# Two layers of cross-attention: three of the six key chunks scored with the keys on the partitions

## The chip, the cores and the metric

The kernel runs on one core of a Trainium2 chip. A NeuronCore has five engines that run side by side and meet through semaphores: PE multiplies matrices (its weight loads are listed apart, as PEld), DVE does elementwise work and reductions, ACT does the exponentials and some copies, POOL issues the stores here, and SP issues the loads. Transfers run on 16 DMA engines. The metric is the device time of one execution in microseconds (us); shorter is better.

## The reference

Two cross-attention layers follow one another over the same context. x is (8, 100, 640), the context is (8, 722, 1024), of which 77 tokens are "text" and 645 are "image" tokens; there are 20 heads of width 32. What one layer computes, for each batch element and head:

```
q = x @ Wq ;  k, v = text @ Wk, text @ Wv ;  ki, vi = image @ Wk_ip, image @ Wv_ip
out_text = softmax(q k^T / sqrt(32)) v
out_ip   = softmax(q ki^T / sqrt(32) [+ 0.5 * sem]) vi   [* mask]
x        = (out_text + out_ip) @ Wo + bo + x
```

What stands in brackets belongs to the second layer alone: sem is a score of the image tokens that all heads share, and mask is a factor for each query row. Everything is float32. Two softmaxes, one over 77 keys and one over 645, are weighted and added.

## The kernel before

**Visits.** A unit u is one batch element of one layer: u = 0 to 7 are the first layer (`B` = 8), 8 to 15 the second. A unit has five chunks c of four heads (4 x 32 = 128 rows of q and k). The main loop, which begins at L1328, makes one visit for each (u, c), 80 in all; the first 40 are the first layer's. A visit makes the scores of its own heads and finishes the heads of the visit before, called `last`.

**Scores (L980).** The 722 keys of a head come in two parts: 512 image keys (`KA`), then 133 image keys and 77 text keys (`KB` = 210 columns). `scores(u, c, 0)` stands at the start of a visit, `scores(u, c, 1)` in its middle. Each makes four matmuls, one for each head, with the head's 32 rows of q as weights and its keys as the moving operand (L992): queries (100) lie on the partitions, keys along the free axis. Four PSUM banks in two tiles `sc0` and `sc1` take them. DVE then takes the maxima (L1001), for part 1 also the text maxima and the shifted text scores (L1022, L1023) and the differences of the two parts' maxima (L1029, L1030). ACT takes the exponentials with their row sums (L1015, two records for each), for part 1 also those of the differences and of the text (L1033, L1034). `factors` on DVE (L1037 to L1041) makes what each part is to be multiplied with, 1/Z included; ACT multiplies the first 512 keys (L1047, one for each head), DVE the remaining ones (L1055 image, L1051 text). The result p of a visit is [100 queries, 4 heads, 722 keys] in SBUF, two buffers.

**Transposes and values.** Before p can be multiplied with v, the keys have to be on the partitions. `transposes` (L1086) does that for one of six chunks of keys j: four transposes on PE into a PSUM bank (L1096), then one copy into `pt`, on DVE (L1103) for j = 0, 1, 3, 5 and on ACT (L1101) for j = 2 and 4. `values` (L1105) makes 24 matmuls with v as weights (L1119) and copies the sum into `hs` (L1123).

**Production.** Between these steps the kernel makes the k and v of later units from the context, by a scheme of seven products instead of eight (`seven`): products a to e go into two PSUM buffers (`ps_pj`), and each is added up by DVE (L207, L217, L222, L228, L233) or copied by ACT (L202, L211). PE can begin a product only when the one that used its buffer two steps earlier has been read. The matmuls are L637 (v) and L667 (k).

**Order.** PE, DVE and ACT run their instructions in the order in which the program writes them (`PINNED`); SP's and POOL's order is left to the scheduler of the framework. `spread` (L1190) gives each production task a place on an axis on which a visit has length 1, from the task's own cost and from a visit's "own" time (5.3 plus small pieces). `between(n, a, b, small)` in the main loop then makes those due between two steps of the visit: 0 to 0.4 before the first two transposes, 0.4 to 0.6 before the next two and part 1, 0.6 to 0.8 before the last two, then the rest. What DVE and ACT do after the maxima is held back in a list `later`; `next_task` (L1298) writes out one entry of it ahead of each production task that has a cost, and the visit's end writes out what is left, ahead of `values`. So in each engine's queue these entries stand between the evictions of production products.

**Loads.** `load_k` fetches the [128, 722] tile of a visit's keys (L507, L508; two buffers), `load_v` its values (L513; two buffers), `load_x` the context (L174), `load_wo` the weights of the output pieces (L895), all on SP.

Of the kernel before, what the change touches and what calls it, by code (L numbers as in the profile page):

```python
# [9 lines left out]
F32 = mybir.dt.float32  # L10
AF = mybir.ActivationFunctionType
ALU = mybir.AluOpType
# [3 lines left out]
B = 8  # L16
# [11 lines left out]
NC_ = C // P  # L28
NCC = CC // P
NTAIL = NL + NT  # L30
SCALE = 1.0 / math.sqrt(D)
SEM_SCALE = 0.5
NU = 2 * B
# [13 lines left out]
def two_layer_xattn(  # L47
# [35 lines left out]
    k_d = [dram.tile([P, NC_, NI], F32, tag=f"k_{u}", name=f"k_d{u}") for u in range(NU)]  # L83
    v_d = [dram.tile([NB * P, C], F32, tag=f"v_{u}", name=f"v_d{u}") for u in range(NU)]
    g_d = [dram.tile([2, NI, NT], F32, tag=f"g_{g}", name=f"g_d{g}") for g in range(B // 2)]

    ident = const.tile([P, P], F32, tag="ident", name="ident")
    make_identity(nc, ident)
# [876 lines left out]
        nc.sync.dma_start(out[LAST[i] % B], resg[g][:, i])  # L965


    pr, stats, sct = {}, {}, {}

    later = []  # L970

# [5 lines left out]

        emit(max([i + 1 for i, (r, _) in enumerate(later) if r], default=0))

    def scores(u, c, part):  # L980
        k0, k1 = ((0, KA), (KA, NK))[part]
        if part == 0:
            pr[u, c] = ppool.tile([S, 4, NK], F32, tag="p", name=f"p_{u}_{c}")

            stats[u, c] = stat.tile([S, 14, 4], F32, tag="st", name=f"st_{u}_{c}")
        else:
            free_scores()

        scs = [ps_sc.tile([P, 2, 512], F32, tag=f"sc{h}", name=f"sc_{u}_{c}_{part}_{h}") for h in range(2)]
        for i in range(4):  # L990
            rows = slice(32 * i, 32 * i + 32)
            nc.tensor.matmul(  # L992
                scs[i // 2][:S, i % 2, : k1 - k0], lhsT=qs_[u][rows, c, :], rhs=ks[u, c][rows, k0:k1], start=True, stop=True
            )
        p, st, l = pr[u, c], stats[u, c], u // B
        n = min(k1, NI) - k0
        lo, f, rz, mul = st[:, 6, :], st[:, 7:9, :], st[:, 9:11, :], st[:, 11:13, :]

        def maxima(h):
            if l == 0:  # L1000
# [31 lines left out]
        def text_exponentials():  # L1032
            nc.scalar.activation(f, f, AF.Exp)  # L1033
            nc.scalar.activation(p[:, :, NI:], p[:, :, NI:], AF.Exp)  # L1034
# [14 lines left out]
        def scaled_rest(text):  # L1049
# [4 lines left out]
            else:  # L1054
# [2 lines left out]
                    ALU.mult,  # L1057
                )

        for h in range(2):  # L1060
            maxima(h)
        if part == 0:
            later.append((True, lambda: exponentials(0)))
            later.append((True, lambda: exponentials(1)))
        else:
            for h in range(2):
                text_maxima(h)
            differences()
            later.append((True, lambda: (exponentials(0), exponentials(1), text_exponentials())))
            if (u, c) == ORDER[-1]:  # L1070

                later.append((False, lambda: (
                    factors(), scaled((0, 1)),
                    nc.vector.tensor_tensor(
                        p[:, 2:, :KA], p[:, 2:, :KA], mul[:, 0, 2:].unsqueeze(2).to_broadcast([S, 2, KA]), ALU.mult
                    ),
                    scaled_rest(False), scaled_rest(True),
                )))
                return
            later.append((False, lambda: (factors(), scaled_rest(False))))  # L1080
            later.append((False, lambda: (scaled((0, 1)), scaled_rest(True))))
            later.append((False, lambda: scaled((2, 3))))

    pts = {}

    def transposes(u, c, j, at_end=False):  # L1086
        if j == 0:
            emit(len(later))
            pts[u, c] = one.tile([P, 6, 4 * S], F32, tag="pt", name=f"pt_{u}_{c}")
        rows = P if j < 5 else NTAIL  # L1090
        if at_end and j in (2, 3):
            ps = ps_sc.tile([P, 2, 512], F32, tag=f"sc{j - 2}", name=f"pspt_{u}_{c}_{j}")[:, 0]
        else:
            ps = ps_pt.tile([P, 512], F32, tag="pt", name=f"pspt_{u}_{c}_{j}")
        for i in range(4):
            nc.tensor.transpose(  # L1096
                ps[:rows, i * S : (i + 1) * S], pr[u, c][:, i, j * P : j * P + rows], ident[:S, :S]
            )
        dst, src = pts[u, c][:rows, j, :], ps[:rows, : 4 * S]
        if j in (2, 4) or at_end and j == 0:  # L1100
            nc.scalar.copy(dst, src)  # L1101
        else:
            nc.vector.tensor_copy(dst, src)  # L1103

    def values(u, c):  # L1105
        g, at = group_of[u]
        if g not in hsg:

            hsg[g] = one.tile([P, 2, NC_, S], F32, tag="hs" if g < len(PAIRS) - 1 else "qst", name=f"hs_{g}")
        pt = pts[u, c]  # L1110
        ps = ps_pt.tile([P, 512], F32, tag="pt", name=f"pv_{u}_{c}")
        for j in range(6):
            for i in range(4):
                if j < 5:
                    lhs = vs[u, c][:, j, i * D : (i + 1) * D]
                else:
                    lhs = vts[u][:, (4 * c + i) * D : (4 * c + i + 1) * D]
                rows = P if j < 5 else NTAIL
                nc.tensor.matmul(  # L1119
                    ps[32 * i : 32 * i + 32, :S], lhsT=lhs, rhs=pt[:rows, j, i * S : (i + 1) * S],  # L1120
                    start=(j == 0), stop=(j == 5),
                )
        nc.vector.tensor_copy(hsg[g][:, at, c, :], ps[:, :S])  # L1123


    AHEAD = 1.2
# [63 lines left out]
    def spread(a, b, tasks):  # L1190

        parts = [(max(a, n), min(b, n + 1)) for n in range(math.floor(a), math.ceil(b))]
        own = [(hi - lo) * (5.3 + small_time(math.floor(lo))) for lo, hi in parts]
        total = sum(t for t, _ in tasks)
        level = (total + sum(own)) / (b - a)
        while True:
            room = [max(0.0, level * (hi - lo) - o) for (lo, hi), o in zip(parts, own)]
            if sum(room) <= total * 1.001:
                break
            level *= 0.999  # L1200
        placed, done, i, before = [], 0.0, 0, 0.0
        scale = sum(room) / total
        for t, f in tasks:
            at = done * scale
            while i < len(parts) - 1 and at >= before + room[i]:
                before += room[i]
                i += 1
            lo, hi = parts[i]
            placed.append((t, lo + (hi - lo) * min(1.0, (at - before) / max(room[i], 1e-9)), f))
            done += t  # L1210
        return placed
# [74 lines left out]
    with tc.manual_schedule(engines=PINNED):  # L1286
# [45 lines left out]
        for n, (u, c) in enumerate(ORDER):  # L1332
# [3 lines left out]
            if n == len(ORDER) - 1:  # L1336
                load_v(*last)
                load_v(u, c)
            between(n, 0.0, 0.4, at[0])
            if last:  # L1340
                transposes(*last, 0)
                transposes(*last, 1)
            between(n, 0.4, 0.6, at[1])
            if last:
                transposes(*last, 2)
                transposes(*last, 3)
            scores(u, c, 1)
            if n == NC_ * LAST[0] - 1:
                load_q(LAST[1])
            few = n >= NC_ * LAST[0] + 4  # L1350
            if not few:
                between(n, 0.6, 0.8, at[2])
            if n < len(ORDER) - 2:
                load_v(u, c)
            if n + 1 < len(ORDER):
                load_k(*ORDER[n + 1])
            if last:
                transposes(*last, 4)
                transposes(*last, 5)
            if few:  # L1360
                between(n, 0.6, 0.8, at[2])
# [58 lines left out]
```

## Time and profile before

| | |
|---|---|
| median of 3 runs | 2047.27 us (2047.24 to 2047.77) |
| the profiled execution | 2048.29 us, of which its trace spans 2046.5 us |
| granted PE clock | 0.998 of full speed |
| PE, PE weight loads, DVE, ACT busy over the span | 99%, 77%, 55%, 38% |
| first visit's scores to those of the 41st (the first layer's visits) | 405.3 to 1338.8 us |
| PE transposes, all visits | 1920, 252 ns each by the records |

A record's duration for PE includes the time in which it overlaps the next one, so a group is better read by the time from its first start to the next group's first start; eight transposes take 0.69 us so. An fp32 matmul of the program shows as two records (a transpose as one). A wait in the table of waits is the idle time of an engine just before an instruction, put down to what ended it. DVE's and ACT's idle time costs nothing by itself as long as PE goes on.

### The profile page before, as it was taken

What the parts mean: (1) busy time and instruction counts of PE and PEld (TensorE: products, weight loads), DVE (VectorE), ACT (ScalarE), POOL (GpSimd) and SP (SyncE); (2) the same over time, 40 slices, a digit from 0 to 9 for tenths busy, and PEclk for the clock granted to TensorE, in tenths of its full rate; (3) what the DMA queues carried; (4) which work ended last, traced back from release to release, by engine and by line L of the source; (5) the groups of instructions that cost most, each with busy time, mean ns of one, the idle gap of its engine ahead of it and who ended that gap; (6) DMA issues with size and microseconds to landing.
All of it is one profiled execution on the core that took longest, in us unless ns stands there. A gap on an engine that the chain in (4) does not pass through costs nothing.

```text
span 2046.5 us, 38708 instructions
## 1 busy us (share of the span) xinstructions
PE 2027.1 (99%) x15162; PEld 1573.3 (77%) x15162; DVE 1130.6 (55%) x3047; ACT 783.0 (38%) x2245; POOL 274.1 (13%) x433
## 2 busy tenths in 40 slices
PE   9999999999999999999999999999999999999998
PEld 9676768776876867778678777777777778888877
DVE  2223322246555455554657665656665667778787
ACT  1001000033433343333434344444543545556675
POOL 0001212111111101111111001001011111111110
PEclk9999999999999999999999999999999999999999
DMA  9544323323432533225245353326332535555461
GB/s 343 151 135 147 102 75 93 99 74 90 117 99 74 155 95 110 86 89 166 79 136 162 106 155 113 95 91 180 107 106 89 152 105 152 161 141 139 124 184 52
DMA packets 296484, 252.20 MB, mean 123 GB/s; under 512 B 46638, under 2 KB 265442, under 8 KB 296302
## 3 DMA queue, kind: packets, MB, share of 16 engines
q1 hardware_dynamic: 274254, 181.19, 31.9%
q0 software_dynamic: 21776, 68.44, 9.2%
q8 instruction: 119, 1.95, 0.4%
q14 instruction: 63, 0.52, 0.1%
q10 hardware_dynamic: 272, 0.10, 0.0%
HBM read 180.74 MB, written 68.93 MB: 122 GB/s over the span
## 4 chain that ended last, share of the span: by engine, by line
PE 95%; DVE 4%; ACT 1%; issue 0%; DMA 0%; SPq 0%; DVEq 0%
PE psv_a L637 9%; PE psv_d L637 8%; PE pspt L1096 8%; PE psk_a L667 8%; PE psk_d L667 7%; PE sc L992 6%; PE pv L1119 4%; PE psv_e L637 4%; PE psk_b L667 4%; PE psk_c L667 4%; PE psv_b L637 4%; PE psv_c L637 4%; PE psk_e L667 4%; PE pso L904 3%; PE psq L923 2%; PE psq L305 2%
## 5 line engine op out<-in xcount | busy, mean ns | idle before, releaser
L1015 ACT ACTIVATE p<-sc,st 100x512 f32<-100x512 f32 (+1 forms) x320 | 165.5, 529 | 202.3 <-DVE st L1001 120.5
L1047 ACT ACTIVATE p<-p,st 100x512 f32<-100x512 f32 x318 | 206.7, 713 | 50.9 <-DVE st L1041 50.6
L1096 PEld LDWEIGHTS pspt<-ident,p 100*128 100x128 f32 (+1 forms) x1920 | 189.0, 138 | 43.3 <-issue 5.5
L1103 DVE COPY pt<-pspt 128x400 f32<-128x400 f32 (+1 forms) x319 | 175.3, 568 | 83.8 <-PE pspt L1096 75.3
L1096 PE MATMUL pspt<-ident,p 100*128 100x100 f32 (+1 forms) x1920 | 211.5, 252 | 6.8 <-DVE pt L1103 2.1
L1015 ACT ACTIVATE p<-p,st 100x512 f32<-100x512 f32 (+1 forms) x320 | 176.6, 554 | 78.2 <-DVE st L1007 78.1
L637 PE MATMUL psv_a<-wv,x 128*128 128x397 f32 (+1 forms) x560 | 185.8, 474 | 0.6 <-DVE ko L228 0.3
L1101 ACT COPY pt<-pspt 128x400 f32<-128x400 f32 x161 | 79.1, 491 | 268.4 <-PE pspt L1096 268.0
L637 PE MATMUL psv_d<-wv,s 128*128 128x320 f32 (+1 forms) x560 | 174.5, 454 | 0.0
L691 POOL DMA_DIRECT2D k_d<-ko x140 | 100.0, 718 | 453.5 <-DVE ko L228 399.8
L637 PEld LDWEIGHTS psv_a<-wv,x 128*128 128x128 f32 x560 | 103.2, 190 | 68.5 <-issue 13.3
L1007 DVE CUSTOM_DVE_ANT_0 p<-sc,sem 100x512 f32<-100x512 f32 (+1 forms) x320 | 138.7, 490 | 21.9 <-PE sc L992 21.0
L637 PEld LDWEIGHTS psv_d<-wv,s 128*128 128x128 f32 x560 | 103.8, 190 | 51.8 <-issue 2.5
L1001 DVE TENSOR_REDUCE st<-sc 100x2 f32<-100x1024 f32 (+1 forms) x160 | 125.3, 824 | 28.8 <-PE sc L992 28.7
L992 PE MATMUL sc<-k,q 32*100 32x210 f32 (+1 forms) x1280 | 138.6, 502 | 0.0
L667 PE MATMUL psk_d<-s,wk 128*128 128x256 f32 (+1 forms) x672 | 136.7, 349 | 0.1
L667 PE MATMUL psk_a<-x,wk 128*128 128x256 f32 (+1 forms) x672 | 135.2, 346 | 0.0
L667 PEld LDWEIGHTS psk_d<-s,wk 128*128 128x128 f32 x672 | 108.6, 189 | 20.6 <-issue 6.7
L667 PEld LDWEIGHTS psk_a<-x,wk 128*128 128x128 f32 x672 | 109.6, 189 | 17.6 <-issue 4.5
L652 POOL DMA_DIRECT2D v_d<-vo x70 | 38.8, 554 | 624.6 <-DVE gst L627 318.6
L637 PE MATMUL psv_e<-wvt,x 128*128 128x397 f32 (+1 forms) x280 | 92.9, 474 | 0.0
L1119 PEld LDWEIGHTS pv<-pt,v 128*32 128x32 f32 x3200 | 67.7, 110 | 26.0 <-issue 16.3
(218 smaller groups left out, 3306.0 us busy)
## 6 DMA issues: line engine op xcount, KB each, us to landing
x<-ip_t SPq DMA_DIRECT2D x80, 512.0 KB
k<-k_d SPq DMA_DIRECT2D x80, 322.5 KB
v<-v_d SPq DMA_DIRECT2D x80, 320.0 KB
v_d<-vo POOLq DMA_DIRECT2D x70, 320.0 KB, 2.4
k_d<-ko POOLq DMA_DIRECT2D x112, 128.0 KB, 4.1
o<-wo SPq DMA_DIRECT2D x35, 320.0 KB
x<-ip_t SPq DMA_DIRECT2D x20, 532.0 KB
q<-wq SPq DMA_DIRECT2D x20, 320.0 KB
```

What stands on the lines that cost most here:

```text
L637: nc.tensor.matmul(ps[:, :m], lhsT=tokens(k)[:, :P], rhs=w[:, k, :], start=(k == 0 and not go_on), stop=(k == HK - 1), skip_group_check=True,)
L667: nc.tensor.matmul(ps[:, i * m : (i + 1) * m], lhsT=w[:, k, :], rhs=tokens(k), start=(i == 0 and k == 0 and not go_on), stop=(k == HK - 1) ...
L691: nc.gpsimd.dma_start(dst[:, :, r], src)
L992: nc.tensor.matmul(scs[i // 2][:S, i % 2, : k1 - k0], lhsT=qs_[u][rows, c, :], rhs=ks[u, c][rows, k0:k1], start=True, stop=True)
L1001: nc.vector.tensor_reduce(st[:, part, 2 * h : 2 * h + 2], scs[h][:S, :, :n], AX.X, ALU.max, negate=True)
L1007: nc.vector.tensor_tensor_reduce(out=p[:, i, k0 : k0 + n], in0=scs[h][:S, i % 2, :n], in1=sems[u][:, k0 : k0 + n], scale=-1.0, scalar=3.0e ...
L1015: nc.scalar.activation(dst, dst if l else scs[h][:S, i % 2, :n], AF.Exp, bias=st[:, part, i : i + 1], scale=-1.0 if l else 1.0, accum_out= ...
L1047: nc.scalar.activation(p[:, i, :KA], p[:, i, :KA], AF.Copy, scale=mul[:, 0, i : i + 1])
L1096: nc.tensor.transpose(ps[:rows, i * S : (i + 1) * S], pr[u, c][:, i, j * P : j * P + rows], ident[:S, :S])
L1101: nc.scalar.copy(dst, src)
L1103: nc.vector.tensor_copy(dst, src)
L1119: nc.tensor.matmul(ps[32 * i : 32 * i + 32, :S], lhsT=lhs, rhs=pt[:rows, j, i * S : (i + 1) * S], start=(j == 0), stop=(j == 5),)
```

## The change

In the first layer, key chunks j = 0, 1, 2 (the first 384 keys, `KT` = 3) are no longer transposed. After part 1 of the next visit's scores, PE makes the scores of `last` for these 384 keys a second time with the operands swapped: k as weights (32 rows x 128 keys), q as the moving operand, so that the keys lie on the partitions (`key_scores`, 12 matmuls). They go into the columns 210 to 509 of the four banks that part 1 of the current heads uses. DVE adds the negative maximum of each query (`key_exponentials`, two instructions) and ACT takes the exponential (two), in place, in `pt`. These come ahead of the current heads' own exponentials in `later`.

The maximum lies along the partitions' other axis, so it goes through DRAM: `finished` writes the smaller of the two negative maxima and 1/Z of each query and head to `st_d` (800 numbers of 4 bytes), and `load_stats` in the next visit reads the first back onto all 128 partitions (as [128, 4, 100]) and the second onto the 32 partitions of each head (four loads), into the tile of p whose first 125 columns are no longer needed. 1/Z is applied after the values: `values` sums chunks 0 to 2 and chunks 3 to 5 into separate columns, and two DVE instructions multiply the first with 1/Z and add the second, in place of one copy.

So for a first-layer visit the four multiplications on ACT fall away (L1047); DVE multiplies columns 384 to 511 instead, in `finished`, which also holds `factors` and the two multiplications that DVE already made, as one entry of `later`. Of the transposes j = 3 and 4 take the place of 0 and 1, those before part 1 fall away, and j = 5 stays. Part 1 moves from 0.6 to 0.5 of the visit, and a first-layer visit's own time in `spread` from 5.3 to 4.8. The second layer is as it was.

```diff
--- before.py
+++ after.py
@@ -28,6 +28,7 @@
 NC_ = C // P
 NCC = CC // P
 NTAIL = NL + NT
+KT = 3
 SCALE = 1.0 / math.sqrt(D)
 SEM_SCALE = 0.5
 NU = 2 * B
@@ -83,6 +84,7 @@
     k_d = [dram.tile([P, NC_, NI], F32, tag=f"k_{u}", name=f"k_d{u}") for u in range(NU)]
     v_d = [dram.tile([NB * P, C], F32, tag=f"v_{u}", name=f"v_d{u}") for u in range(NU)]
     g_d = [dram.tile([2, NI, NT], F32, tag=f"g_{g}", name=f"g_d{g}") for g in range(B // 2)]
+    st_d = [dram.tile([2, 4, S], F32, tag=f"st_{i}", name=f"st_d{i}") for i in range(2)]
 
     ident = const.tile([P, P], F32, tag="ident", name="ident")
     make_identity(nc, ident)
@@ -965,7 +967,7 @@
         nc.sync.dma_start(out[LAST[i] % B], resg[g][:, i])
 
 
-    pr, stats, sct = {}, {}, {}
+    pr, stats, wholes = {}, {}, {}
 
     later = []
 
@@ -977,10 +979,12 @@
 
         emit(max([i + 1 for i, (r, _) in enumerate(later) if r], default=0))
 
-    def scores(u, c, part):
+    def scores(u, c, part, keys_of=None):
+
         k0, k1 = ((0, KA), (KA, NK))[part]
         if part == 0:
-            pr[u, c] = ppool.tile([S, 4, NK], F32, tag="p", name=f"p_{u}_{c}")
+            wholes[u, c] = ppool.tile([P, 4, NK], F32, tag="p", name=f"p_{u}_{c}")
+            pr[u, c] = wholes[u, c][:S]
 
             stats[u, c] = stat.tile([S, 14, 4], F32, tag="st", name=f"st_{u}_{c}")
         else:
@@ -992,9 +996,11 @@
             nc.tensor.matmul(
                 scs[i // 2][:S, i % 2, : k1 - k0], lhsT=qs_[u][rows, c, :], rhs=ks[u, c][rows, k0:k1], start=True, stop=True
             )
+        if keys_of:
+            key_scores(*keys_of, scs)
         p, st, l = pr[u, c], stats[u, c], u // B
         n = min(k1, NI) - k0
-        lo, f, rz, mul = st[:, 6, :], st[:, 7:9, :], st[:, 9:11, :], st[:, 11:13, :]
+        lo, f, rz, mul = st[:, 8, :], st[:, 6:8, :], st[:, 9:11, :], st[:, 11:13, :]
 
         def maxima(h):
             if l == 0:
@@ -1056,6 +1062,17 @@
                     p[:, :, KA:NI], p[:, :, KA:NI], mul[:, 1, :].unsqueeze(2).to_broadcast([S, 4, NI - KA]),
                     ALU.mult,
                 )
+
+        def finished():
+
+            factors()
+            nc.vector.tensor_tensor(
+                p[:, :, KT * P : KA], p[:, :, KT * P : KA],
+                mul[:, 0, :].unsqueeze(2).to_broadcast([S, 4, KA - KT * P]), ALU.mult,
+            )
+            scaled_rest(False)
+            scaled_rest(True)
+            nc.sync.dma_start(st_d[(NC_ * u + c) % 2].rearrange("r i q -> q r i"), st[:, 8:10, :])
 
         for h in range(2):
             maxima(h)
@@ -1066,7 +1083,12 @@
             for h in range(2):
                 text_maxima(h)
             differences()
+            if keys_of:
+                later.append((True, lambda: [key_exponentials(*keys_of, scs, h) for h in range(2)]))
             later.append((True, lambda: (exponentials(0), exponentials(1), text_exponentials())))
+            if l == 0:
+                later.append((False, finished))
+                return
             if (u, c) == ORDER[-1]:
 
                 later.append((False, lambda: (
@@ -1083,8 +1105,37 @@
 
     pts = {}
 
+    def load_stats(u, c):
+
+        whole, src = wholes[u, c], st_d[(NC_ * u + c) % 2]
+        nc.sync.dma_start(whole[:, :, :S], src[0].unsqueeze(0).to_broadcast([P, 4, S]))
+        for i in range(4):
+            nc.sync.dma_start(
+                whole[32 * i : 32 * i + 32, :, S : S + S // 4],
+                src[1, i].rearrange("(a q) -> a q", a=4).unsqueeze(0).to_broadcast([32, 4, S // 4]),
+            )
+
+    def key_scores(u, c, scs):
+
+        for j in range(KT):
+            for i in range(4):
+                rows = slice(32 * i, 32 * i + 32)
+                nc.tensor.matmul(
+                    scs[i // 2][:, i % 2, KB + j * S : KB + (j + 1) * S], lhsT=ks[u, c][rows, j * P : (j + 1) * P],
+                    rhs=qs_[u][rows, c, :], start=True, stop=True,
+                )
+
+    def key_exponentials(u, c, scs, h):
+        dst = pts[u, c][:, :KT, 2 * h * S : 2 * (h + 1) * S]
+        nc.vector.tensor_tensor(
+            dst.rearrange("p j (i q) -> p i j q", q=S),
+            scs[h][:, :, KB : KB + KT * S].rearrange("p i (j q) -> p i j q", q=S),
+            wholes[u, c][:, 2 * h : 2 * h + 2, :S].unsqueeze(2).to_broadcast([P, 2, KT, S]), ALU.add,
+        )
+        nc.scalar.activation(dst, dst, AF.Exp)
+
     def transposes(u, c, j, at_end=False):
-        if j == 0:
+        if (u, c) not in pts:
             emit(len(later))
             pts[u, c] = one.tile([P, 6, 4 * S], F32, tag="pt", name=f"pt_{u}_{c}")
         rows = P if j < 5 else NTAIL
@@ -1109,6 +1160,8 @@
             hsg[g] = one.tile([P, 2, NC_, S], F32, tag="hs" if g < len(PAIRS) - 1 else "qst", name=f"hs_{g}")
         pt = pts[u, c]
         ps = ps_pt.tile([P, 512], F32, tag="pt", name=f"pv_{u}_{c}")
+
+        apart = u < B
         for j in range(6):
             for i in range(4):
                 if j < 5:
@@ -1116,11 +1169,20 @@
                 else:
                     lhs = vts[u][:, (4 * c + i) * D : (4 * c + i + 1) * D]
                 rows = P if j < 5 else NTAIL
+                q0 = S if apart and j >= KT else 0
                 nc.tensor.matmul(
-                    ps[32 * i : 32 * i + 32, :S], lhsT=lhs, rhs=pt[:rows, j, i * S : (i + 1) * S],
-                    start=(j == 0), stop=(j == 5),
-                )
-        nc.vector.tensor_copy(hsg[g][:, at, c, :], ps[:, :S])
+                    ps[32 * i : 32 * i + 32, q0 : q0 + S], lhsT=lhs, rhs=pt[:rows, j, i * S : (i + 1) * S],
+                    start=(j == 0 or apart and j == KT), stop=(j == 5 or apart and j == KT - 1),
+                )
+        hs = hsg[g][:, at, c, :]
+        if apart:
+            nc.vector.tensor_tensor(
+                hs.rearrange("p (a q) -> p a q", a=4), ps[:, :S].rearrange("p (a q) -> p a q", a=4),
+                wholes[u, c][:, :, S : S + S // 4], ALU.mult,
+            )
+            nc.vector.tensor_tensor(hs, hs, ps[:, S : 2 * S], ALU.add)
+        else:
+            nc.vector.tensor_copy(hs, ps[:, :S])
 
 
     AHEAD = 1.2
@@ -1190,7 +1252,7 @@
     def spread(a, b, tasks):
 
         parts = [(max(a, n), min(b, n + 1)) for n in range(math.floor(a), math.ceil(b))]
-        own = [(hi - lo) * (5.3 + small_time(math.floor(lo))) for lo, hi in parts]
+        own = [(hi - lo) * ((4.8 if lo < NC_ * B else 5.3) + small_time(math.floor(lo))) for lo, hi in parts]
         total = sum(t for t, _ in tasks)
         level = (total + sum(own)) / (b - a)
         while True:
@@ -1336,26 +1398,30 @@
             if n == len(ORDER) - 1:
                 load_v(*last)
                 load_v(u, c)
+            first = last and last[0] < B
+            if first:
+                load_stats(*last)
             between(n, 0.0, 0.4, at[0])
             if last:
-                transposes(*last, 0)
-                transposes(*last, 1)
-            between(n, 0.4, 0.6, at[1])
-            if last:
+                transposes(*last, KT if first else 0)
+                transposes(*last, KT + 1 if first else 1)
+            between(n, 0.4, 0.5 if first else 0.6, at[1])
+            if last and not first:
                 transposes(*last, 2)
                 transposes(*last, 3)
-            scores(u, c, 1)
+            scores(u, c, 1, last if first else None)
             if n == NC_ * LAST[0] - 1:
                 load_q(LAST[1])
             few = n >= NC_ * LAST[0] + 4
             if not few:
-                between(n, 0.6, 0.8, at[2])
+                between(n, 0.5 if first else 0.6, 0.8, at[2])
             if n < len(ORDER) - 2:
                 load_v(u, c)
             if n + 1 < len(ORDER):
                 load_k(*ORDER[n + 1])
             if last:
-                transposes(*last, 4)
+                if not first:
+                    transposes(*last, 4)
                 transposes(*last, 5)
             if few:
                 between(n, 0.6, 0.8, at[2])
```

## The prediction

> **What bounds the kernel now.** I read the page's busy shares and its chain of work first, then the busy times of one stretch, then the order of time within one visit.
>
> ```profile
> PE 2027.1 (99%) x15162; PEld 1573.3 (77%) x15162; DVE 1130.6 (55%) x3047; ACT 783.0 (38%) x2245; POOL 274.1 (13%) x433
> ...
> PE 95%; DVE 4%; ACT 1%; issue 0%; DMA 0%; SPq 0%; DVEq 0%
> ```
>
> PE is the bound: what PE saves is saved, and what makes PE wait is lost. The stretch that the change touches, the first layer's 40 visits:
>
> ```profile
> 405.30:1338.80 933.50, 932.38 (x6746) 708.17 (x6745) 527.86 (x1239) 370.59 (x1087) 126.03 (x202) 1.00 0.38 110
> ```
>
> Columns: stretch, its length, busy PE, PE loads, DVE, ACT, POOL, clock, DMA share, GB/s. 933.5 / 40 = 23.3 us a visit. Taking for each product the time from its first matmul to the next product's, and what is over the usual value, I find PE's waits in it to be 3 to 5 us in all. So there is nothing to gain from waits, only from PE work, and any new wait is a loss. One middle of a visit (the visit of unit 3, chunk 0) in order of time, merged rows, start and length first:
>
> ```profile
> 772.50 0.62 PE L992 MATMUL sc<-k,q 32*100 32x210 f32 x8
> 773.04 2.00 PE L667 MATMUL psk_d<-s,w 128*128 128x256 f32 x8
> 773.15 0.78 DVE L1001 TENSOR_REDUCE st<-sc 100x2 f32<-100x266 f32 x2
> 774.88 1.89 PE L667 MATMUL psk_a<-x,wk 128*128 128x256 f32 x8
> 775.27 0.42 DVE L233 TENSOR_TENSOR ko<-psk_d,ko 128x256 f32<-128x256 f32 x1
> 776.10 0.47 ACT L1034 ACTIVATE p<-p 100x308 f32<-100x308 f32 x1
> 776.59 0.47 DVE L1037 TENSOR_REDUCE st<-p 100x4 f32<-100x308 f32 x1 [0.91 <-ACT p L1034]
> 777.87 0.71 DVE L1055 TENSOR_TENSOR p<-p,st 100x532 f32<-100x532 f32 x1
> 778.34 0.85 PE L1096 MATMUL pspt<-ident,p 100*128 100x100 f32 x8
> 778.89 0.42 DVE L207 TENSOR_TENSOR ko<-psk_b,ko 128x256 f32<-128x256 f32 x1
> 779.03 1.92 PE L667 MATMUL psk_a<-x,wk 128*128 128x256 f32 x8
> ```
>
> DVE stands still 0.91 us for ACT's last exponential and then runs `factors` (L1037 to 777.84) and two multiplications, and only then evicts product b (L207), which PE had finished at 778.34. PE needs that buffer two products later. Here it all just fits.
>
> **What the Trainium skill says.** "TensorE: Matmul & The Clock Gate", LDWEIGHTS: a weight load lasts columns / 1.2 ns, whatever the rows: 107 ns for 128 columns, 83 for 100. The trace agrees: two loads of a product start 108 ns apart, and in part 0's scores four loads start within 20 ns (four row groups at once) and the next four 83 ns later, while the first matmuls run. "TensorEngine Tiling (Array Packing)", Key Properties: changing the tiling mode drains PE. Part 1 takes 0.54 us where two passes of 210 columns cost 2 x 0.175, so a part of the rest is that; the key scores stay in the mode and pay no second one. "PSUM — Partial Sum Buffer", bank collisions: two engines may not touch one bank at a time, readers included, so the program must order them. The table of waits shows it: ACT's part 1 exponentials, which need nothing from L1023, wait 79.6 us for it over 39 times. The same page, Engine vs sequencer instructions: DVE and ACT are strict FIFO. The 0.91 us above show it.
>
> **PE's part.** Removed for each visit: 12 transposes, 1.5 groups of eight at 0.688 us (778.34 to 779.03) = 1.03 us. Added: 12 matmuls with 100 moving columns, six rounds (three chunks, two passes) of four row groups at once. A round's matmuls last 2 x 100 / 2.4 = 83 ns (a transpose of as many columns takes 0.688 / 8 = 86), its loads 107, so loads set the pace; the first hides under part 1's second pass. 5 x 107 + 83 = 0.62 us. Bounds: 0.50 if the matmuls set the pace; 1.14 if a load can't overlap its own row group's matmul (six times 190), which the 83 ns above speak against. Saved: 0.41 us a visit, 40 visits: 16.6 us (21 to -4).
>
> **DVE and ACT.** From rows of DVE with one PSUM operand (256 columns 421 ns, 320 columns 490) an element costs 1.08 ns: the two additions of 600 columns take 0.80 us each. ACT's exponential of 308 columns takes 0.47; at 0.83 ns an element (688 at 512, 370 at 133) 600 take 0.70. `finished` adds 512 columns on DVE, 0.69 (532 take 0.71). `values` ends with two DVE instructions of 0.26. DVE: +1.60 +0.69 +0.26 -2 x 0.57 (copies of j = 0 and 1; the one of 3 stays) = +1.4 us a visit; ACT: +1.40 -4 x 0.71 -0.49 = -1.9. By totals both have room (DVE 57% busy). By order they have not. I follow the same visit after the change, time 0 at part 1's start; part 1 comes one to two products earlier, at 0.5.
>
> - PE: part 1 and keys to 1.16, products X1 (e) to 3.09, X2 (d again) to 4.82.
> - DVE waits for the key scores too (same banks), starts at 1.26; maxima, text, differences take 2.2 as above: 3.5. The additions are ahead of X1 in `later`: to 5.1. X1's eviction to 5.5, X2's to 5.9. Product X3 wants X1's buffer at 4.82, gets it at 5.6: PE loses 0.8.
> - ACT: key exponentials to 5.9, then part 1's, which take 2.0 (774.60 to 776.57): 7.9. In the kernel before this ended at 4.1.
> - DVE: `factors`, written out ahead of X3, waits until 7.9, 1.25 long: 9.2; three multiplications 1.87: 11.1; product X4's eviction to 11.5. X4 was done at 9.1. PE makes the last transposes and X5 until 11.25 and X6 must wait 0.3 more.
>
> PE loses 1.1 us and saves 0.4. I filled in such a table for all 40 visits, with the planner's places of the products as the code gives them and these durations. For the kernel before it gives 934 us (trace: 933.5), 5 us of them PE waits, and single visits within about 1 us of the trace, so I trust it. After: 18 visits lose 1 to 4 us each (those with k products in the second half, 1.73 us each: two of them are shorter than DVE's delay; a v product of 2.2 to 2.7 covers more), the rest almost nothing; 40 us in all. Sum: -16.6 + (40 - 5) + about 26 restarts that show a first weight load (0.1 each) = +21 us. If DVE need not wait for the key scores it is +10; with key scores at 0.50, +17.
>
> **Transfers.** SP gets six more issues a visit at 0.3 to 0.5 us. The write of 800 single numbers makes one descriptor each ("DMA: Bandwidth & Descriptors", Rules for kernel authors; no run shows one; an estimate from its 2 us fixed cost and 9 ns for the smallest packets in the trace is 3 us, with tens of ns each perhaps 8), the loads (400-byte packets, 24 ns here) some 4 us. From `factors` to the next additions there are, by the same table, 10 to 12 us in the three shortest visits and 14 to 20 in the rest: covered up to 10 us, +2 more at 12 and +22 at 16, because additions waiting on DVE hold evictions back. k tiles: their buffer is now freed by the key scores, half a visit before the load is used, where it was one and a half (packets land 20 to 35 us ahead of use). Issue to last packet is 2.4 to 6 us, the second half 8 to 15: hidden but for 1 us perhaps in the shortest visits. SP's other loads don't wait for new things unless they stand behind these; SP's order isn't pinned.
>
> **Time.** Against the profiled execution: 2048.3 + 21 = 2069.3; it is 1.0 over the median, so 2068 for the median.
>
> **Rivals.**
> 1. *PE's saving survives* (faster). The place is the eviction behind `finished`: if it ends within two products (some 9 us instead of 11.5) PE never waits, and 2047.3 - 16.6 = 2031; at 0.50 us for the keys, 2026. For it: DVE and ACT have room in total. Against it: the 4 us by which the chain of additions and exponentials is longer are all in order ahead of `factors`. With half the waits it is near 2047.
> 2. *Key scores don't overlap loads* (1.14 us): +42 in my table, 2089. Against it: the loads 83 ns apart.
> 3. *The statistics come late*: 16 us from `factors` to their landing gives 2090, 20 us some 2175. For it: the single-number write; one DMA queue shared with loads of 512 KB. Against: packets of the trace are short.
>
> **Chances.** As forecast 0.58 (its own range 2055 to 2085, from +10 and +35 with late loads); rival 1 0.20; rival 2 0.08; rival 3 0.14. A measurement here can tell 0.2%, 4 us: faster 0.17, same 0.06 (both within rival 1 and the forecast's lower edge), slower 0.77. The range leaves out half of rival 1 and the late end of rival 3: 2036 to 2100.
>
> **What would show it.** The time from part 1's first matmul to the next product's: 1.16 us if the keys are costed right. DVE's additions at 0.80, and DVE idle ahead of L1037's successor for ACT. Waits of k products on DVE's evictions (L207 to L233), in pairs, some 40 us. PE's busy time over the 40 visits would hide the waits only in part: their length should be 955. I am wrong if the products follow without gaps (then rival 1), if DVE's additions wait for a DMA (rival 3), or if PE waits at part 0 for k.

## The result, and the profile after

The changed kernel takes 2071.45 us (median of 4 runs, 2070.75 to 2072.93), the kernel before 2047.52 (4 runs); the ratio is 1.0118, with a 95% interval of 1.0100 to 1.0135. It is slower by 24 us; 2068 us had been forecast. The profiled execution spans 2069.7 us, 23.2 more than that of before, and 22.8 of it lie in the 40 visits of the first layer. Their length, from the first scores of visit 0 to those of visit 40, is 956.4 us; it was 933.6 (forecast: 955).

The page of the changed kernel, busy shares and the chain that ended last:

```profile
PE 2023.6 (98%) x15642; PEld 1560.7 (75%) x15642; DVE 1174.0 (57%) x3127; ACT 716.0 (35%) x2125; POOL 274.9 (13%) x433
...
PE 60%; DVE 6%; DMA 3%; ACT 2%; issue 1%; SPq 0%; ACTq 0%; DVEq 0%
```

PE is busy for less time than before (2023.6 for 2027.1 us) in a span that is longer, and the chain, which ran over PE for 95%, now goes through DVE, ACT and transfers again and again (the shares shown add up to 72%; the rest of the span is not resolved). Busy times of the stretch of 40 visits (columns: stretch, length, PE, PE loads, DVE, ACT, POOL, clock, DMA share, GB/s):

```profile
405.57:1361.98 956.41, 929.82 (x7215) 697.75 (x7214) 570.86 (x1317) 301.47 (x966) 126.42 (x202) 1.00 0.51 118
```

PE's idle time in the stretch (its length less PE's busy time) was 933.5 - 932.4 = 1 us and is now 956.4 - 929.8 = 27 us. The same visit that the prediction followed (unit 3, chunk 0), in order of time; start and length in us:

```profile
776.58 0.61 PE L996 MATMUL sc<-k,q 32*100 32x210 f32 x8
777.02 0.82 PE L1123 MATMUL sc<-q,k 32*128 32x100 f32 x24
777.77 2.00 PE L669 MATMUL psk_e<-x,w 128*128 128x256 f32 x8
777.88 0.78 DVE L1007 TENSOR_REDUCE st<-sc 100x2 f32<-100x266 f32 x2 [0.76 <-PE sc L1123]
...
780.00 1.46 DVE L1130 TENSOR_TENSOR pt<-sc,p 128x600 f32<-128x600 f32 x2
780.81 1.39 ACT L1135 ACTIVATE pt<-pt 128x600 f32<-128x600 f32 x2 [5.38 <-DVE pt L1130]
781.38 0.41 DVE L230 TENSOR_TENSOR ko<-psk_e,ko 128x256 f32<-128x256 f32 x1
...
781.85 2.00 PE L669 MATMUL psk_a<-x,wk 128*128 128x256 f32 x8 [0.35 <-DVE ko L230]
...
783.60 0.47 ACT L1040 ACTIVATE p<-p 100x308 f32<-100x308 f32 x1
...
784.10 0.47 DVE L1043 TENSOR_REDUCE st<-p 100x4 f32<-100x308 f32 x1 [1.98 <-ACT p L1040]
...
785.38 0.69 DVE L1069 TENSOR_TENSOR p<-p,st 100x512 f32<-100x512 f32 x1
785.99 0.71 DVE L1061 TENSOR_TENSOR p<-p,st 100x532 f32<-100x532 f32 x1
786.61 0.47 DVE L1057 TENSOR_TENSOR p<-p,st 100x308 f32<-100x308 f32 x1
787.00 0.42 DVE L209 TENSOR_TENSOR ko<-psk_b,ko 128x256 f32<-128x256 f32 x1
```

Read it against the prediction's list, time 0 at 776.58. Part 1 and the key scores last 1.19 us (forecast 1.16). DVE does wait for the key scores and starts at 1.30 (1.26). The additions are over at 4.9 (5.1), the key exponentials ahead of part 1's on ACT, whose last text exponential ends at 7.5 (7.9). DVE stands 1.98 us for it at L1043, the first line of `factors`; the multiplications end at 10.5 (11.1) and the eviction behind them at 10.8 (11.5). PE stands 0.35 us for L230 (forecast 0.8). The order is as forecast; the steps on DVE and ACT are a little shorter.

What the forecast did not have is in the same trace. SP's own waits over these 40 visits (waiter, releaser, us in all, times, longest):

```profile
SPq L1111 <- DMA st_d<-st: 266.5, 40, 9.5
SPq L1075 <- DVE st L1047: 220.2, 40, 33.6
```

SP issues the load of the statistics (L1111) only when their write has landed, stands there for 266.5 us in all, and whatever is behind it stands too. (It stands nearly as long at the write itself, L1075, which waits for `factors`.) Visit 32 and visit 34, in order of time:

```profile
1184.74 0.32 SPq L1075 DMA_DIRECT2D st_d<-st  x1
1185.15 2.47 SPq L515 DMA_DIRECT2D v<-v_d  x1
1195.31 0.36 SPq L1111 DMA_DIRECT2D p<-st_d  x1
1195.72 3.04 SPq L1113 DMA_DIRECT2D p<-st_d  x4
1198.86 0.96 SPq L897 DMA_DIRECT2D q<-wq  x2
...
1204.30 3.60 PE L925 MATMUL psq<-res,q 128*128 128x200 f32 x10 [4.13 <-DMA q<-wq]
...
1246.05 1.47 DVE L1130 TENSOR_TENSOR pt<-sc,p 128x600 f32<-128x600 f32 x2 [2.31 <-DMA p<-st_d]
...
1248.63 4.11 PE L639 MATMUL psv_d<-wv,s 128*128 128x320 f32 x8 [2.10 <-ACT vo L213]
```

In the first, two loads of the next layer's query weights go out behind the statistics at 1198.86, and PE waits 4.1 us for them. In the second, a short visit, the additions themselves wait for the statistics, ACT's key exponentials with them, and PE for an eviction on ACT.

### The profile page after: what moved, and what is told of

It reads as the page before. It is cut to its first block, busy times and chain, and to the rows that moved or that the text cites. A ratio compares the mean times of both kernels' runs of the same rounds, so it can differ in the third digit from the quotient of the medians.

```text
span 2069.7 us, 40047 instructions
## 1 busy us (share of the span) xinstructions
PE 2023.6 (98%) x15642; PEld 1560.7 (75%) x15642; DVE 1174.0 (57%) x3127; ACT 716.0 (35%) x2125; POOL 274.9 (13%) x433
## 4 chain that ended last, share of the span: by engine, by line
PE 60%; DVE 6%; DMA 3%; ACT 2%; issue 1%; SPq 0%; ACTq 0%; DVEq 0%
PE psv_d L639 5%; PE psv_a L639 5%; PE pspt L1147 5%; PE psk_a L669 5%; PE sc L996 5%; PE psk_d L669 4%; PE pv L1173 4%; PE pso L906 3%; PE psv_e L639 3%; PE psv_c L639 2%; PE psk_b L669 2%; PE psk_c L669 2%; PE psv_b L639 2%; PE psk_e L669 2%; PE psq L925 1%; DMA st_d<-st 1%
## 5 line engine op out<-in xcount | busy, mean ns | idle before, releaser
L1154 DVE COPY pt<-pspt 128x400 f32<-128x400 f32 x239 | 132.9, 568 | 71.8 <-PE pspt L1147 69.7
L1147 PEld LDWEIGHTS pspt<-ident,p 100*128 100x128 f32 (+1 forms) x1440 | 141.9, 137 | 37.4 <-issue 4.9
L1147 PE MATMUL pspt<-ident,p 100*128 100x100 f32 (+1 forms) x1440 | 162.4, 251 | 6.9 <-DVE pt L1154 2.1
L1135 ACT ACTIVATE pt<-pt 128x600 f32<-128x600 f32 x80 | 55.8, 705 | 228.7 <-DVE pt L1130 228.7
L669 PEld LDWEIGHTS psk_d<-s,wk 128*128 128x128 f32 x672 | 108.0, 189 | 27.1 <-DVE ko L224 5.4
L1152 ACT COPY pt<-pspt 128x400 f32<-128x400 f32 x121 | 59.5, 492 | 191.6 <-PE pspt L1147 191.5
L1053 ACT ACTIVATE p<-p,st 100x512 f32<-100x512 f32 x158 | 102.9, 715 | 27.4 <-DVE st L1047 27.1
```

What stands on the lines that cost most here:

```text
L669: nc.tensor.matmul(ps[:, i * m : (i + 1) * m], lhsT=w[:, k, :], rhs=tokens(k), start=(i == 0 and k == 0 and not go_on), stop=(k == HK - 1) ...
L1053: nc.scalar.activation(p[:, i, :KA], p[:, i, :KA], AF.Copy, scale=mul[:, 0, i : i + 1])
L1147: nc.tensor.transpose(ps[:rows, i * S : (i + 1) * S], pr[u, c][:, i, j * P : j * P + rows], ident[:S, :S])
```

## The experiments

All lengths "of the 40 visits" are from the first scores of visit 0 to those of visit 40; visits count from 0. "The table" is the prediction's: each instruction in its engine's order, starting when its engine is free and what it reads is ready.

### Part 1's exponentials first

```diff
-            if keys_of:
-                later.append((True, lambda: [key_exponentials(*keys_of, scs, h) for h in range(2)]))
             later.append((True, lambda: (exponentials(0), exponentials(1), text_exponentials())))
+            if keys_of:
+                later.append((True, lambda: [key_exponentials(*keys_of, scs, h) for h in range(2)]))
```

> Part 1's exponentials ahead of the key additions and key exponentials, nothing else changed. My theory (the 2.9 us of additions and key exponentials lie in order ahead of `factors`, and DVE's stand there is what delays the evictions): the in-order table of the prediction, with the measured 0.645 us for the key scores and 0.77 us for an addition, gives 931 us for the 40 visits instead of 955, so 956 - 24 = 932 in the trace and 2048 us for the run (2042 to 2055). Rival, transfers (statistics, loads behind them on SP): the order on ACT matters little, 2066 or more. Rival, PE's own work: no change, 2071.

Measured: 2045.54 us (12 runs), ratio to the kernel before 0.9990 (0.9981 to 0.9998); 40 visits 932.1 us. The same visit of this kernel:

```profile
768.15 0.61 PE L996 MATMUL sc<-k,q 32*100 32x210 f32 x8
...
771.89 1.46 DVE L1130 TENSOR_TENSOR pt<-sc,p 128x600 f32<-128x600 f32 x2
...
772.40 0.47 ACT L1040 ACTIVATE p<-p 100x308 f32<-100x308 f32 x1
772.75 1.34 ACT L1135 ACTIVATE pt<-pt 128x600 f32<-128x600 f32 x2
772.90 1.89 PE L669 MATMUL psk_a<-x,wk 128*128 128x256 f32 x8
...
773.60 0.47 DVE L1043 TENSOR_REDUCE st<-p 100x4 f32<-100x308 f32 x1
```

ACT's last text exponential now ends 4.7 us after part 1's start instead of 7.5, DVE reaches L1043 without standing for ACT, and PE's product (772.90) has no wait. The same instructions, two entries of a list exchanged: 26 us. That the order in the list makes this difference is shown; how much of it comes by way of the transfers, the third experiment tells.

### Statistics that are there already

```diff
+    st_0 = dram.tile([2, 4, S], F32, tag="st_0", name="st_0")
...
+    nc.sync.dma_start(st_0.rearrange("r i q -> (r i) q"), ident[S : S + 8, :S])
...
-        whole, src = wholes[u, c], st_d[(NC_ * u + c) % 2]
+        whole, src = wholes[u, c], st_0
```

> The statistics are read from a DRAM tile of zeros written once at the start, so their load waits for no write of this visit; the write stays (the output is then not the reference's: the shift and the factor of the three key chunks are zero). My theory: only the waits that the trace shows on transfers go (PE for k 2.2 us, PE for the q weights 4.1 and 1.7 behind it, the two visits in which the additions waited for the statistics some 4 us): 2060 to 2066. Rival, transfers as the main cause: about 2047. If SP's stand at the statistics costs nothing: 2071.

Measured: 2056.91 us, ratio 1.0047 (1.0030 to 1.0064); 40 visits 941.8 us, 14.6 less than the changed kernel, where 8 were expected. The transfers cost nearly twice what I had read off the waits. A part of the difference is PE's clock. In the changed kernel it was granted at half speed for some 3.4 us, twice in the 40 visits, just after the two waits shown above (4.13 us before 1204.30, 2.10 before 1248.63). The columns of the first two lines are those of the stretch above (the clock is the last but two); the third is the group of ten matmuls that stood 4.13 us there, in this kernel, where it did not wait:

```profile
1204.30:1207.80 3.50, 3.50 (x11) 3.50 (x12) 0.00 (x0) 0.00 (x0) 0.00 (x0) 0.51 1.16 318
1248.60:1252.10 3.50, 3.47 (x7) 2.30 (x8) 1.86 (x7) 1.86 (x10) 0.00 (x0) 0.52 0.03 7
```

```profile
1196.00 1.85 PE L927 MATMUL psq<-res,q 128*128 128x200 f32 x10
```

Here the next group starts 1.69 us after it, in the changed kernel 3.39 us. So this wait cost 4.1 us and 1.7 more; with the second one, the clock makes 3.5 of the 14.6 us. With ready statistics no such stretch is left in the 40 visits. Four visits hold 13.9 of the 14.6 us:

```
visit    before   changed   statistics ready   their loads on POOL   exponentials first
3         22.4      23.4         22.0                22.0                 22.2
28        23.2      25.1         22.8                22.8                 22.8
32        27.7      33.1         27.0                27.5                 33.8
34        16.0      21.9         17.8                22.1                 15.7
```

### Both

The two edits above together.

> Both edits: part 1's exponentials first, statistics from a tile written at the start (output not the reference's, as in the run with this edit alone). My theory: the two add up, 2048 - 8 = 2040 us (2034 to 2046), 924 us for the 40 visits. Rival, transfers alone: the same as with the ready statistics alone. If one hides the other: no lower than the lower of the two single runs.

Measured: 2038.99 us, ratio 0.9961 (0.9946 to 0.9976); 40 visits 924.9 us. As expected. The order is worth 24.3 us with late statistics (956.4 - 932.1) and 16.9 with ready ones (941.8 - 924.9): some 7 of the transfers' 14.6 go with the order alone. The likely reason is that `factors`, and with it the write of the statistics, is two us earlier in the visit. Visits 28 and 34 in the last column of the table are where it shows. Visit 32 stays.

### `factors` and the multiplications in two entries

```diff
+        def ready():
+            factors()
+            nc.sync.dma_start(st_d[(NC_ * u + c) % 2].rearrange("r i q -> q r i"), st[:, 8:10, :])
...
+                later.append((False, ready))
                 later.append((False, finished))
```

`finished` keeps the three multiplications; the order of the first experiment stays.

> Part 1's exponentials first, and `factors` (with the write of the statistics) one entry of `later`, the three multiplications the next, so that an eviction comes between them. My theory: DVE's block of 3.1 us becomes 1.25 and 1.87, the table gives 928.4 us instead of 931.2 for the 40 visits, 2045 us (2040 to 2052). Rival, transfers: no change from the order alone.

Measured: 2044.94 us (12 runs), ratio 0.9985 (0.9977 to 0.9994); 40 visits 931.3 us. Against the order alone that is 0.8 us in the profile and 0.6 in the medians: no difference that can be told. The block of 3 us is covered once it comes early enough; the table's 2.8 us were not there.

### The loads of the statistics on POOL

```diff
-        nc.sync.dma_start(whole[:, :, :S], src[0].unsqueeze(0).to_broadcast([P, 4, S]))
+        nc.gpsimd.dma_start(whole[:, :, :S], src[0].unsqueeze(0).to_broadcast([P, 4, S]))
```

and the four loads after it in the same way; everything else as in the changed kernel.

> The changed kernel with the loads of the statistics issued by POOL instead of SP; nothing else moves. It tells SP's standing at these loads apart from the statistics' own lateness. My theory: the k load (2.3 us) and the q weights (6.0 us) that were late behind SP's stand come in time, the additions of the one short visit still wait (4 us): 2061 to 2066. Rival, the statistics' own lateness is what costs: 2071 or more. Rival, POOL's writes of k and v were not covered: more than 2071, with waits on ko and vo.

Measured: 2060.58 us, just below the range expected, ratio 1.0062 (1.0045 to 1.0078); 40 visits 947.0 us, 9.4 less than the changed kernel. The table of four visits shows where: visits 3, 28 and 32 are as with ready statistics, visit 34 is not. So of the transfers' 14.6 us some 9 are SP's stand at the load, which held up other loads, and some 4 the statistics' own lateness, the slower clock after the waits included in both. SP's stand at the write is as long as before (223.8 us), so it is not what cost the 9. POOL, which now stands 225 us for the write, has the room.

### PE's part alone, nearly

```diff
-        nc.vector.tensor_tensor(
-            dst.rearrange("p j (i q) -> p i j q", q=S),
-            scs[h][:, :, KB : KB + KT * S].rearrange("p i (j q) -> p i j q", q=S),
-            wholes[u, c][:, 2 * h : 2 * h + 2, :S].unsqueeze(2).to_broadcast([P, 2, KT, S]), ALU.add,
-        )
-        nc.scalar.activation(dst, dst, AF.Exp)
+        nc.scalar.activation(
+            dst.rearrange("p j (i q) -> p i j q", q=S),
+            scs[h][:, :, KB : KB + KT * S].rearrange("p i (j q) -> p i j q", q=S), AF.Exp,
+        )
...
-            nc.scalar.activation(f, f, AF.Exp)
+            both = st[:, 6:9, :] if l == 0 else f
+            nc.scalar.activation(both, both, AF.Exp)
...
+            nc.vector.tensor_tensor(lo, lo, rz[:, 0, :], ALU.mult)
```

The key exponentials stay ahead of part 1's here: without the additions they need nothing from DVE.

> The key scores are exponentiated without the shift (valid where scores stay under some 80): ACT reads them from PSUM directly, DVE's two additions go, exp(lo) goes into the one factor that is read at the visit's end, and only that half of the statistics goes through DRAM, with its load after the next k load. `factors` and the three multiplications are two entries. PE's instructions are those of the changed kernel, so this is its saving with the chain and the transfers taken away. My theory: 40 visits of 918 us by the table (933.5 - 15.5 saved, waits as before), 2031 us (2026 to 2037). Rival: if PE's saving of 0.39 us a visit isn't real, or if DVE's `finished` alone holds the evictions up, 2045 or more.

Measured: 2039.14 us, ratio 0.9957 (0.9943 to 0.9972); 40 visits 926.2 us instead of 918. A miss by 8 us, and 7 of them are one visit: visit 32 took 34.1 us, because its q weights still stand behind a load of the statistics (L1117 in this kernel) on SP, which SP reaches ahead of them although it is written out later. The other waits of PE of more than 0.2 us are four, 2.0 us in all. That led to the next two.

### Two versions with the loads on POOL

First the one that keeps the shift: part 1's exponentials first, two entries, the loads of the statistics on POOL.

> Part 1's exponentials first, `factors` and the multiplications in two entries, and the loads of the statistics issued by POOL; the softmax shift stays. My theory: the last large loss of the run with the first two edits is the q weights behind SP's stand (visit 32: 33.8 us, 27.0 with ready statistics); on POOL it goes, 931 - 7 = 924 us for the 40 visits and 2038 us (2033 to 2043). Rival, the statistics come late on POOL behind its writes of k and v: 2045 or more.

Measured: 2039.10 us (5 runs), ratio 0.9961 (0.9946 to 0.9975); 40 visits 926.5 us, visit 32 at 27.1. It keeps all of the change's arithmetic and is faster than the changed kernel and the one before.

Then the version without the shift, with its loads on POOL.

> The run without the shift, with the loads of the statistics issued by POOL. My theory: its one large loss (visit 32: 34.1 us where 27 is the work) goes, 926 - 7 = 919 us for the 40 visits, as the table has it (918), and 2032 us (2028 to 2037): the saving on PE that the prediction counted, at last. Rival, POOL too late: 2039 or more, with DVE's last multiplication of the values waiting for the statistics.

Measured: 2034.35 us, ratio 0.9939 (0.9923 to 0.9955); 40 visits 920.4 us, visit 32 at 27.0. It is the fastest here, for scores that stay under some 80. Its page, and the two largest waits of PE's matmuls in the 40 visits (waiter, releaser, us in all, times, longest):

```profile
PE 2011.1 (99%) x15642; PEld 1558.4 (77%) x15642; DVE 1119.5 (55%) x3087; ACT 710.0 (35%) x2125; POOL 363.3 (18%) x593
...
PE 92%; DVE 4%; DMA 1%; ACT 1%; issue 1%; POOL 0%; DVEq 0%; ACTq 0%; POOLq 0%; SPq 0%
```

```profile
PE psv_a L639 <- DVE ko L230: 1.4, 2, 0.7
PE psk_a L669 <- ACT ko L204: 0.4, 1, 0.4
```

PE runs the same 15642 matmuls as in the changed kernel and is 37 us sooner done. PE's saving is real; it was spent on waits.

### Part 1 where it was

```diff
-        own = [(hi - lo) * ((4.8 if lo < NC_ * B else 5.3) + small_time(math.floor(lo))) for lo, hi in parts]
+        own = [(hi - lo) * (5.3 + small_time(math.floor(lo))) for lo, hi in parts]
...
-            between(n, 0.4, 0.5 if first else 0.6, at[1])
+            between(n, 0.4, 0.6, at[1])
```

> The changed kernel with the planner's numbers of the kernel before: part 1 at 0.6 of the visit instead of 0.5, 5.3 us reserved instead of 4.8. The table gives 957.9 us for the 40 visits instead of 954.8 (the later start leaves the same chain less room before the values): 2071.5 + 3 = 2074 us. If the earlier start was itself the loss (less cover ahead of the additions), it would be under 2065; if the place doesn't matter, 2071.

Measured: 2066.68 us, but the four times lie between 2060.89 (granted clock 1.000) and 2073.20 (0.994), so they tell little; the profiled execution has 952.4 us for the 40 visits, 4.0 less than the changed kernel. The visits 3, 28, 32 and 34 make up -5.3 of it (statistics that meet other moments); the rest is +1.3, in the direction and near the size of the table's +3. The place of part 1 isn't what made the change slow.

### Who has to wait at a bank

```diff
-        if keys_of:
-            key_scores(*keys_of, scs)
         p, st, l = pr[u, c], stats[u, c], u // B
...
             differences()
             if keys_of:
+                key_scores(*keys_of, scs)
                 later.append((True, lambda: [key_exponentials(*keys_of, scs, h) for h in range(2)]))
```

> The changed kernel with the key scores written out after part 1's maxima and text operations instead of ahead of them; PE's order is the same, the words only decide who waits for whom. If the order is needed because the regions lie in the same banks (the prediction's reading): PE now waits for DVE's 2.2 us at each of the 39 key scores, 80 to 90 us more, 2150 to 2165. If only overlapping regions wait: DVE starts 0.65 us earlier and the table gives -10, 2061.

Measured: 2162.52 us (2 runs), ratio 1.0566 (1.0533 to 1.0598); 40 visits 1047.1 us. In order of time, the visit of unit 3, chunk 0, and then the stretch of the 40 visits (busy PE after its length, granted clock in the last but two column):

```profile
808.36 0.61 PE L996 MATMUL sc<-k,q 32*100 32x210 f32 x8
809.01 0.78 DVE L1005 TENSOR_REDUCE st<-sc 100x2 f32<-100x266 f32 x2
...
810.41 1.49 PE L1122 MATMUL sc<-q,k 32*128 32x100 f32 x24 [1.44 <-DVE p L1027]
```

```profile
405.77:1452.86 1047.09, 984.25 (x7215) 730.37 (x7214) 576.42 (x1317) 303.03 (x966) 125.94 (x202) 0.96 0.46 108
```

DVE starts 0.65 us after part 1 instead of 1.30, and now PE waits for DVE's last reading of the bank. Reads and writes of different columns are kept apart here; the program's order only says who waits. Whether they are kept apart by the bank or by the tile of two banks, this run does not tell. Of the 91 us that the 40 visits grew, 36 are idle time of PE (62.8 instead of 26.6 us, 60 of it ahead of the key scores) and 54 are busy time. The lower clock, 0.96 where the changed kernel has 1.00, is most of the latter: the trace has 23 stretches of 3.4 us at half speed in the 40 visits, together some 39 us lost.

## Why the prediction was right, and where it was not

The time (2068 against 2071.45), the direction and the length of the 40 visits (955 against 956.4) came out. The sum behind them did not come out term by term:

```
                                       forecast    measured
PE's work, 40 visits                    -16.6       -15.5    (1.03 removed, 0.64 added a visit)
waits by order, restarts with them      +37.6       +23.7    (941.8 - 933.6 + 15.5, statistics ready)
transfers                                +0.0       +14.6    (956.4 - 941.8)
40 visits                               954.5       956.4
```

Two errors of 14 us cancelled, which is luck. (The transfers are taken away first here, because the forecast's table has none; with the order mended first they cost 7.2.) So the number proves less than it seems to, and the steps have to be judged one by one.

- *PE's saving.* Right. Part 1's first matmul to the next product's is 1.188 us, forecast 1.16; the key scores add 0.64 us where 0.62 were costed. The weight loads start in fours some 111 ns apart, not the 190 ns of a load and a matmul one after the other, so they set the pace and overlap their own row group's matmuls. Rival 2 (1.14 us) is out. The visits show the saving as it is: thirteen of the changed kernel's 40 are 0.38 to 0.39 us shorter than before, visit 8 with 23.37 instead of 23.75 and visit 21 with 28.91 instead of 29.30 (forecast 0.41). One reading of the prediction is off: the second four loads of part 0's scores start 85 ns after the first in its trace, not 83. That a drain between tiling modes is a part of part 1's 0.54 us is shown by no run.
- *DVE and ACT.* Right in size: an addition takes 0.774 us (0.80), a key exponential 0.705 (0.70).
- *The order.* Right in kind, and shown: `factors` stands behind ACT, evictions stand behind the additions and behind `finished`, and exchanging two entries took 24 us off the 40 visits. That the table gave 24 as well is luck again: it has no late transfers, and without them the exchange was worth 16.9 of the 23.7 us. The other 6.8 stay with the order mended (924.9 against 933.6 - 15.5). That DVE waits for the key scores ahead of it in its own banks is shown as well, by the last experiment. The prediction's sign for the banks, ACT's 79.6 us behind L1023, settles less, because these two instructions also write to one tile, p.
- *The waits' size.* Too large, by 14 us with the restarts. With ready statistics ten visits are 1.0 to 2.5 us longer than their length before less the 0.39 saved, 19 us together; 18 visits that lose 1 to 4 us were forecast. The table put the durations of records end to end. In the trace above the multiplications start at 785.38, 785.99 and 786.61 and the eviction at 787.00, each some 0.08 us before the record ahead of it ends (0.61 us for a record of 0.69). With it, and with shorter steps on ACT, the chain of the visit shown takes 10.8 us instead of 11.5. The Trainium skill says it, in "Perfetto Trace Analysis", Optimizing Scalar/DVE Operations: about half of the fixed part of a profiled DVE instruction, the write's acknowledgement, overlaps with the next instruction. I had not used it. With 0.05 us taken off every DVE instruction the table gives 942 for the changed kernel with ready statistics (941.8) and 923 with the exponentials first (924.9); with the 0.08 of the trace 936 and 920. The overlap is seen in the trace; that it makes up the whole of the 14 us is a calculation with a fitted value and not shown by a run.
- *Transfers.* This is the step that failed. The forecast put it at nothing. Rival 3 asked whether the statistics reach the additions in time, and all but 4 of the 80 additions found them there (4.3 us); the sentence that failed is the one on SP: other loads don't wait "unless they stand behind these". They do stand behind these. The write lands 6 to 11 us after its issue (the time between the issues of L1075 and L1111), SP stands at L1111 for it in 40 visits, and k and q weights behind it came late: 9 us, as the run with the loads on POOL shows. "DMA: Bandwidth & Descriptors", Two DMAs through the same engine are not ordered, has the rule: the issuing engine has to wait for the first transfer's semaphore before it issues the second. The 266.5 us above agree. The estimate of 3 to 8 us for the write was short by up to 3 us: six of the 40 writes took 9.7 to 11.3 us, and these are the ones in whose first 6 us packets of 0.9 to 1.7 MB set out.
- *Rival 1*, PE's saving survives: false for this kernel, and true of what it could be. Its 2031 us needed the evictions to be freed of the chain and SP of the round trip, and with both, and the additions gone, 2034 was reached.

## What to carry to other kernels

When a change gives an engine in the background more to do, follow the order on each engine through one visit, and look first at what of the new work has to be ahead of the old: two entries of a list were worth 24 us here, as much as the whole loss (some 7 of them because the statistics were then written earlier). A value that goes out to memory and back stopped the queue that issued its second half; put that half on a queue on which nothing urgent is behind it. And when a forecast comes out right, set its terms against measurements of each before trusting the method that gave it.

## What was not expected of the hardware

- PE's granted clock fell after waits of PE. In the changed kernel it was at half speed for 3.4 us right after the waits of 4.1 and 2.1 us, and at full speed in the rest of the 40 visits. With a wait of 1.1 to 1.6 us ahead of the key scores of every visit (the last experiment) it was at half speed in 23 stretches of 3.4 us, each beginning 0.7 to 2.4 us after such a wait ended; the mean was 0.96 over the 40 visits (1.00 before) and 0.979 over the run. So a wait of PE cost more than its own length here, some 1.7 us for each stretch. Why some of the waits brought one and others did not is not shown.
- The four runs of the kernel with part 1 at 0.6 differ by 0.6%, and their clocks, 1.000 to 0.994, by as much; the runs of each other kernel lie within 0.45% of each other.
- A write of 800 single numbers took 6.2 to 11.3 us from its issue to its landing.
